# The values of self-attention in PE tiles of 64 rows by 32 columns

## Chip, cores and metric

The kernel runs on one core of a Trainium2 chip. The metric is device time in microseconds (us) of one execution, lower is better. All data is float32.

## What is computed

A transformer block over `x` of 2 x 1024 x 256: self-attention, cross-attention over a context of 154 tokens, and a gated feed-forward, each behind a layer norm and with a residual. There are 16 heads of width 64. Only the self-attention matters here:

```python
def _attention(xq, xkv, wq, wk, wv, wo, bo):
    q = (xq @ wq).reshape(B, S, N_HEADS, D_HEAD)
    k = (xkv @ wk).reshape(B, T, N_HEADS, D_HEAD)
    v = (xkv @ wv).reshape(B, T, N_HEADS, D_HEAD)
    attn = jnp.einsum("bihd,bjhd->bhij", q, k) * D_HEAD ** (-0.5)
    attn = jax.nn.softmax(attn, axis=-1)
    out = jnp.einsum("bhij,bjhd->bihd", attn, v).reshape(B, S, D_ATTN)
    return out @ wo + bo
h = _layernorm(x, ln1_g, ln1_b)
x = _attention(h, h, sa_wq, sa_wk, sa_wv, sa_wo, sa_bo) + x
```

## The kernel before

The order of all work is written out by hand, instruction by instruction and per engine; each engine works its own list in order and waits on semaphores.

**Units and slots.** Self-attention is cut into 16 units, each a pair of heads of one batch (`units`, L578). A unit has eight slots, 128 in all: the loop `for p in range(SA)` (L1036 to L1070) takes one slot per turn. In each slot TensorE does first two score tiles (`self_first`, L637, which calls `scores`, L476) and then one more piece of work from a list.

**Scores.** A score tile is 128 partitions x 2 heads x 512 keys in PSUM, `s`; the pool `ps_s` has two of them. The partitions are four groups of 32, for two groups of 32 queries and two halves of the keys. TensorE works here as eight small arrays (tiles) side by side, each of 64 rows by 32 columns: 64 rows because a head is 64 wide, two row groups for the two heads, four column groups for the four groups of partitions. The tile is set by `tile_position=(j * DH, a4 * KB)` (L486). The projections of queries and keys (`project_both`, L345, lines 352 in the profile, tiles `pq_sa`, `pk_sa`) have the same shape in this stage, since they are called with `m=KB`, 32 columns.

**Softmax.** DVE takes the negative maximum of a score tile (L645, `st`), ACT the exponentials with their sums (L494, `p`). The two halves of the keys exchange maxima and sums by small DMAs within SBUF (`exchange`, L500, `st<-st`), GpSimd joins them (`join`, L508, up to `den`), DVE takes the reciprocal (L591, `rd`) and GpSimd scales `p` with it (L595). DVE then transposes `p` in blocks of 32 x 32 into `pT` (L609, `turn_groups`, two slots later).

**The values weighed.** Four slots of a unit are followed by a call of `self_values` (L613), two for each half of the 1024 queries. It calls `weigh` (L523) for four of the eight tiles `t` of keys; two calls make one half. `weigh` multiplies the values `v` (stationary) with `pT` (moving, 256 queries at a time) and sums over all keys into two PSUM banks, `po[0]` and `po[1]`. Keys lie 64 to a row group (`a2`); `e` selects the copy of the values in which the two row groups are exchanged, so that each row group serves both banks' keys in turn. In the profile this is line 530, tiles `po`, `pT`, `v_sa`. ACT copies the finished banks to `o_sa` (L630).

**Other pieces.** The other four slots of a unit carry the projection of the next unit's queries (`pq_sa`), keys (`pk_sa`) and values (L383, `pv_sa`, tiles of 64 rows by 128 columns), and a piece of the output projection (L457, `py_sa`, whole array of 128 x 128). Transposes of layer norms (`ph_ln`) ride along in some slots. Self-attention ends near 713 us; cross-attention follows (its scores `sc`, L772, its values `poc`, L851, in tiles of 64 x 64), and the feed-forward (`pa`, L933, `pf`, L956). Two calls of `self_values` fall in the first slots of cross-attention (L1117 to L1120).

A call of `nc.tensor.matmul` on float32 data is recorded as two pairs of a weight load (LDWEIGHTS, row PEld) and a matmul (row PE): the 2048 calls of `weigh` are the 4096 loads and 4096 matmuls of line 530.

Of the kernel before, what the change touches and what calls it, by code (L numbers as in the profile page):

```python
# [18 lines left out]
def tile_transformer_block(ctx: ExitStack, tc: tile.TileContext, a: dict, out: bass.AP):  # L19
# [8 lines left out]
    DH = 64  # L28
# [11 lines left out]
    KB = 32  # L40
# [3 lines left out]
    QG = 2 * KB  # L44
    TP = NB * KB
    NM = P // QG
    QH = S // 2
    GH = QH // QG
    NK = HB // KB
# [45 lines left out]
    row_of, r = {}, 0  # L95
# [427 lines left out]
    def weigh(po, v, pT, t):  # L523

        for e in range(2):
            for a2 in range(2):
                r = slice(a2 * QG, (a2 + 1) * QG)
                n = 2 * t + (e ^ a2)
                for j in range(2):
                    nc.tensor.matmul(  # L530
                        po[a2][j * DH:(j + 1) * DH, :QH // 2],
                        lhsT=v[r, t, e, j * DH:(j + 1) * DH], rhs=pT[r, j * NK + n, :],
                        start=(t == 0 and e == 0), stop=(t == NT - 1 and e == 1),
                        tile_position=(a2 * QG, j * DH),
                    )


# [75 lines left out]
    def self_values(h, part):  # L613

        b, pr = units[h // 2]
        if part == 0:
            bank = sum_tile if h < 2 * NU - 1 else mm_tile
            halves[h, "po"] = [bank(f"po_{h}_{a2}") for a2 in range(2)]
            if pr % HP == 0 and h % 2 == 0:
                oT["sa", b, pr // HP] = pt_.tile([P, HP, S], F32, tag="oT", name=f"o_sa{b}_{pr}")  # L620
        po = halves[h, "po"]
        for t in range(NT // 2 * part, NT // 2 * (part + 1)):
            weigh(po, qk["sa", b, pr][2], halves[h], t)
        if part == 0:
            return None
        dst = oT["sa", b, pr // HP][:, pr % HP, (h % 2) * QH:(h % 2 + 1) * QH]

        def store():
            for a2 in range(2):
                nc.scalar.copy(  # L630
                    dst.rearrange("p (g a i) -> p g a i", a=2, i=KB)[:, :, a2, :],
                    po[a2][:, :QH // 2].rearrange("p (g i) -> p g i", i=KB),
                )

        return store
# [342 lines left out]
    with tc.manual_schedule():  # L978
# [57 lines left out]
        for p in range(SA):  # L1036
# [21 lines left out]
            if h == 0 or hg < LAG:  # L1058
# [4 lines left out]
                ui, n = divmod(p, 2 * SH)  # L1063
# [8 lines left out]
        for c in range(CA):  # L1072
# [13 lines left out]
            ui, n = divmod(c, len(CG))  # L1086
# [125 lines left out]
```

## Time and profile before

| What | us |
|---|---|
| median of 3 runs | 1120.16 (1119.69 to 1120.71) |
| the profiled execution | 1119.22 |
| its span, first to last instruction | 1117.4 |
| TensorE matmul busy | 1103.5 |
| VectorE (DVE) busy | 855.7 |
| ScalarE (ACT) busy | 629.5 |
| GpSimd (POOL) busy | 681.0 |
| line 530, matmuls of `po`, busy (4096) | 235.8 |
| line 483, matmuls of the scores, busy (4096) | 251.6 |

A row of the profile names line, engine, operation and tiles (written <- read). For TensorE it gives the shape of the PE tile first, rows*columns (64*64), and then partitions x elements of the moving operand (64x256). Behind the bar stand the busy time of the group in us, the mean length of one in ns, and the idle time of the engine just ahead of it with what ended it. Matmuls side by side in different tiles overlap, so the busy time of a group is far less than its count by its mean. The ends of matmuls are modelled; their starts are recorded, so the pace of TensorE is read from start to start. The granted TensorE clock was 1.00 over the whole span.

### The profile page before, as it was taken

What the parts mean: (1) busy time and instruction counts of PE and PEld (TensorE: products, weight loads), DVE (VectorE), ACT (ScalarE), POOL (GpSimd) and SP (SyncE); (2) the same over time, 40 slices, a digit from 0 to 9 for tenths busy, and PEclk for the clock granted to TensorE, in tenths of its full rate; (3) what the DMA queues carried; (4) which work ended last, traced back from release to release, by engine and by line L of the source; (5) the groups of instructions that cost most, each with busy time, mean ns of one, the idle gap of its engine ahead of it and who ended that gap; (6) DMA issues with size and microseconds to landing.
All of it is one profiled execution on the core that took longest, in us unless ns stands there. A gap on an engine that the chain in (4) does not pass through costs nothing.

```text
span 1117.4 us, 36668 instructions
## 1 busy us (share of the span) xinstructions
PE 1103.5 (99%) x14340; PEld 686.5 (61%) x14340; DVE 855.7 (77%) x1205; ACT 629.5 (56%) x2030; POOL 681.0 (61%) x1584
## 2 busy tenths in 40 slices
PE   8999999999999999999999999999999999999998
PEld 5445545545545455455455455476776777888887
DVE  4889999898998899999989989868777875412212
ACT  4666666766666666667666765665555553121111
POOL 2777777777777777777777777766656653220000
PEclk9999999999999999999999999999999999999999
DMA  3222212111111012011111111146665453000000
GB/s 85 70 57 50 55 27 51 48 34 41 32 31 42 22 41 46 13 42 39 24 41 32 31 32 26 25 95 158 160 157 125 114 115 79 10 11 10 20 10 19
DMA packets 102318, 59.14 MB, mean 53 GB/s; under 512 B 31994, under 2 KB 92930, under 8 KB 102146
## 3 DMA queue, kind: packets, MB, share of 16 engines
q1 hardware_dynamic: 100914, 56.15, 21.3%
q8 instruction: 113, 1.85, 0.7%
q10 hardware_dynamic: 1232, 0.66, 0.2%
q14 instruction: 59, 0.48, 0.1%
HBM read 27.12 MB, written 2.10 MB: 26 GB/s over the span
## 4 chain that ended last, share of the span: by engine, by line
PE 92%; ACT 2%; DVE 2%; DMA 1%; POOL 1%; SPq 1%; issue 1%; DVEq 0%; ACTq 0%; POOLq 0%
PE s L483 20%; PE po L530 20%; PE pa L933 10%; PE py_sa L457 5%; PE pv_sa L383 5%; PE py_ca L457 5%; PE pf L956 5%; PE pk_sa L352 4%; PE pq_sa L352 4%; PE pq_ca L352 4%; PE poc L851 4%; PE sc L772 3%; ACT p L494 2%; PE ph_ln L270 1%; PE pv_ca L733 1%; DVE st L645 1%
## 5 line engine op out<-in xcount | busy, mean ns | idle before, releaser
L494 ACT ACTIVATE p<-s,st 128x512 f32<-128x512 f32 x512 | 344.8, 686 | 199.0 <-DVE st L645 190.6
L595 POOL TENSOR_SCALAR p<-p,rd,ee 128x512 f32<-128x512 f32 x512 | 385.6, 768 | 47.6 <-DVE rd L591 46.3
L645 DVE TENSOR_REDUCE st<-s 128x2 f32<-128x1024 f32 x256 | 301.1, 1217 | 26.9 <-PE s L483 13.5
L609 DVE STREAM_TRANSPOSE pT<-p 128x1024 f32<-128x1024 f32 x256 | 302.2, 1218 | 0.3 <-POOL p L595 0.3
L483 PE MATMUL s<-k_sa,q_sa 64*32 64x512 f32 x4096 | 251.6, 594 | 5.0 <-ACT p L494 4.3
L530 PE MATMUL po<-pT,v_sa 64*64 64x256 f32 x4096 | 235.8, 380 | 0.9 <-DVE pT L609 0.9
L530 PEld LDWEIGHTS po<-pT,v_sa 64*64 64x64 f32 x4096 | 150.6, 133 | 109.3 <-issue 31.2
L483 PEld LDWEIGHTS s<-k_sa,q_sa 64*32 64x32 f32 x4096 | 66.8, 106 | 126.3 <-issue 68.2
L799 POOL TENSOR_SCALAR p<-p,rden 128x154 f32<-128x154 f32 x256 | 96.8, 399 | 76.0 <-DVE rden L796 75.6
L788 ACT ACTIVATE p<-sc,neg 128x154 f32<-128x154 f32 x256 | 96.1, 405 | 83.3 <-DVE rden L796 78.1
L942 DVE SCALAR_TENSOR_TENSOR u<-pa,cols,gate 128x256 f32<-128x256 f32 x64 | 31.0, 484 | 123.1 <-ACT gate L939 123.1
L933 PE MATMUL pa<-hT_ln,wf 128*128 128x256 f32 x512 | 121.1, 380 | 0.2 <-ACT p L788 0.2
L939 ACT ACTIVATE gate<-pa,cols 128x256 f32<-128x256 f32 x64 | 30.3, 474 | 147.8 <-PE pa L933 146.0
L933 PEld LDWEIGHTS pa<-hT_ln,wf 128*128 128x128 f32 x512 | 96.9, 190 | 13.9 <-issue 0.8
L494 ACT ACTIVATION_READ_ACCUMULATOR p<-s,st 128x1 f32 x512 | 103.8, 203 | 0.0
L383 PEld LDWEIGHTS pv_sa<-sa_wv,hT_ln 64*128 64x128 f32 x1024 | 58.8, 188 | 14.5 <-DMA st<-st 5.9
L518 POOL TENSOR_TENSOR zz<-ee,st 128x8 f32<-128x8 f32 x128 | 25.9, 202 | 65.6 <-ACT ee L516 65.6
L956 PE MATMUL pf<-wf,u 128*128 128x256 f32 x256 | 64.7, 379 | 0.0
L383 PE MATMUL pv_sa<-sa_wv,hT_ln 64*128 64x128 f32 x1024 | 62.0, 276 | 0.2 <-ACT v_sa L392 0.2
L457 PE MATMUL py_sa<-sa_wo,o_sa 128*128 128x256 f32 x256 | 59.7, 386 | 0.0
L457 PE MATMUL py_ca<-ca_wo,o_ca 128*128 128x256 f32 x256 | 59.7, 382 | 0.0
L457 PEld LDWEIGHTS py_sa<-sa_wo,o_sa 128*128 128x128 f32 x256 | 47.4, 190 | 17.8 <-issue 6.2
(87 smaller groups left out, 1250.6 us busy)
## 6 DMA issues: line engine op xcount, KB each, us to landing
wf<-pT_ca SPq DMA_DIRECT2D x128, 128.0 KB, 2.4
st<-st SPq DMA_DIRECT2D x512, 1.0 KB, 1.8
v_sa<-v_sa SPq DMA_DIRECT2D x32, 256.0 KB, 3.5
sa_wq<-in_L_xattn_sa_wq_dram SPq DMA_DIRECT2D x32, 128.0 KB, 2.8
sa_wk<-in_L_xattn_sa_wk_dram SPq DMA_DIRECT2D x32, 128.0 KB, 2.9
sa_wv<-in_L_xattn_sa_wv_dram SPq DMA_DIRECT2D x32, 128.0 KB, 2.9
ca_wq<-in_L_xattn_ca_wq_dram SPq DMA_DIRECT2D x32, 128.0 KB, 3.3
wf<-in_L_xattn_ff_w_dram SPq DMA_DIRECT2D x12, 256.0 KB, 4.2
```

What stands on the lines that cost most here:

```text
L352: nc.tensor.matmul(pq[r][f:f + m, at:at + n], lhsT=wt[own, c, f:f + m], rhs=h[own, c, t0:t0 + n], start=(c == 0), stop=(c == NH - 1), tile ...
L383: nc.tensor.matmul(pv[r][:, i * P:(i + 1) * P], lhsT=h[own, c, i * P:(i + 1) * P], rhs=wt[own, c, :], start=(c == 0), stop=(c == NH - 1), ...
L457: nc.tensor.matmul(py[:, e * D:(e + 1) * D], lhsT=o[:, i, (t + e) * P:(t + e + 1) * P], rhs=wo[kind][:, g * HP + i, :], start=(i == 0), st ...
L483: nc.tensor.matmul(sc[a4 * KB:(a4 + 1) * KB, j, :], lhsT=q[r, c:c + KB], rhs=k[r, h * HB:(h + 1) * HB], start=True, stop=True, tile_positi ...
L494: nc.scalar.activation(pr[:, j, :], sc[:, j, :], AF.Exp, bias=st[:, 0, 0, i, j:j + 1], accum_out=st[:, 0, 1, i, j:j + 1],)
L530: nc.tensor.matmul(po[a2][j * DH:(j + 1) * DH, :QH // 2], lhsT=v[r, t, e, j * DH:(j + 1) * DH], rhs=pT[r, j * NK + n, :], start=(t == 0 an ...
L595: nc.gpsimd.tensor_scalar(pr[:, j, :], pr[:, j, :], rd[:, c:c + 1], ee[:, 0, c:c + 1], op0=ALU.mult, op1=ALU.mult,)
L609: nc.vector.transpose(halves[h][:, :, c:c + KB], groups.pop(0).rearrange("p j (n k) -> p (j n) k", k=KB))
L645: nc.vector.tensor_reduce(st[:, 0, 0, i, :], sc[i], AX.X, ALU.max, negate=True)
L799: nc.gpsimd.tensor_scalar(pr_[:, j, i, :T], pr_[:, j, i, :T], rden[:, j, i:i + 1], 1.0, op0=ALU.mult, op1=ALU.mult,)
L933: nc.tensor.matmul(pa[:, half, :TF * P], lhsT=w1[:, c, half * DF + f * P:half * DF + (f + 1) * P], rhs=h[:, c, t0 * P:(t0 + TF) * P], star ...
L956: nc.tensor.matmul(sums[blk][i][:, :D], lhsT=sums[blk, "u"][:, f, i * P:(i + 1) * P], rhs=w2[:, f, :], start=(f == 0), stop=(f == NF - 1),)
```

## The change

Each call of `weigh` had stationary values of 64 rows by 64 columns, one head, and four tiles of the array were in use at once, 64*64. Now the 64 columns of a head are cut in two: a call takes 32 columns of `v`, streams the same `pT` of its head (`d // DH`), and writes 32 partitions of `po[a2]`. So there are twice as many calls, eight tiles of 64*32. The sums, the PSUM banks, the data and what comes before and after stay.

```diff
             for a2 in range(2):
                 r = slice(a2 * QG, (a2 + 1) * QG)
                 n = 2 * t + (e ^ a2)
-                for j in range(2):
+                for d in range(0, 2 * DH, KB):
                     nc.tensor.matmul(
-                        po[a2][j * DH:(j + 1) * DH, :QH // 2],
-                        lhsT=v[r, t, e, j * DH:(j + 1) * DH], rhs=pT[r, j * NK + n, :],
+                        po[a2][d:d + KB, :QH // 2],
+                        lhsT=v[r, t, e, d:d + KB], rhs=pT[r, d // DH * NK + n, :],
                         start=(t == 0 and e == 0), stop=(t == NT - 1 and e == 1),
-                        tile_position=(a2 * QG, j * DH),
+                        tile_position=(a2 * QG, d),
                     )
```

(`KB` is 32, `DH` 64, `QG` 64, `QH` 512, `NK` 16, `NT` 8.)

## The prediction

> **What bounds the kernel now.** I read the page first (sections 1, 4, 5), then the chain of waits between 400 and 440 us, then busy time by stretch, the waits of the self-attention stage, and the start of the first scores.
>
> ```profile
> PE 1103.5 (99%) x14340; PEld 686.5 (61%) x14340; DVE 855.7 (77%) x1205; ACT 629.5 (56%) x2030; POOL 681.0 (61%) x1584
> ...
> L645 DVE TENSOR_REDUCE st<-s 128x2 f32<-128x1024 f32 x256 | 301.1, 1217 | 26.9 <-PE s L483 13.5
> L609 DVE STREAM_TRANSPOSE pT<-p 128x1024 f32<-128x1024 f32 x256 | 302.2, 1218 | 0.3 <-POOL p L595 0.3
> L483 PE MATMUL s<-k_sa,q_sa 64*32 64x512 f32 x4096 | 251.6, 594 | 5.0 <-ACT p L494 4.3
> L530 PE MATMUL po<-pT,v_sa 64*64 64x256 f32 x4096 | 235.8, 380 | 0.9 <-DVE pT L609 0.9
> L530 PEld LDWEIGHTS po<-pT,v_sa 64*64 64x64 f32 x4096 | 150.6, 133 | 109.3 <-issue 31.2
> L483 PEld LDWEIGHTS s<-k_sa,q_sa 64*32 64x32 f32 x4096 | 66.8, 106 | 126.3 <-issue 68.2
> ```
>
> TensorE is busy 99% of the span and has almost no idle time before the changed line (0.9 us) or the scores (5.0). What the array does back to back sets the end; a busy array can still lose time inside its busy time, though. For that, the chain of waits (columns: start, length, engine, tile, line, matmuls):
>
> ```profile
> 16 pieces in order of time: start us, us, what
> ...
> 411.97 1.88 PE s L483 x32
> 413.85 3.43 PE pq_sa L352 x64
> 417.28 1.72 PE s L483 x32
> 419.00 3.43 PE pk_sa L352 x64
> 422.43 1.72 PE s L483 x32
> 424.14 3.62 PE po L530 x64
> 427.76 1.88 PE s L483 x32
> ```
>
> The same 32 score matmuls take 1.72 us behind a projection in the same 64*32 shape, and 1.88 behind `po`, which is in 64*64. And `po` itself takes 3.62 where `pq_sa`, with as many columns through each tile (8 x 512 against 16 x 256), takes 3.43. Round by round in the trace: score rounds (eight matmuls side by side) follow each other at 429 ns; the last before `po` lasts 566 and the first behind it 453. Rounds of `po` (four side by side) follow at 216; its first lasts 266, its last 325 to 327. So one visit to `po` costs 137 + 50 + 110 + 24 = 321 ns beyond its rounds, paid only at the change of shape: between scores and `pq_sa` or `pk_sa` every round is 428 to 430.
>
> **The change, part by part.** *Counts.* `weigh` makes 2048 calls, each recorded as two loads and two matmuls (4096 in the rows). After: 4096 calls, 8192 loads and 8192 matmuls, half as wide in weights, each still streaming 256 columns. A visit becomes 128 matmuls in 16 rounds of eight instead of 64 in 16 rounds of four. Banks, accumulation, the waits on `pT` and the ACT copies (L630) stay.
>
> *Removed.* The trace has 64 visits; 62 follow a score piece, 61 are followed by one. Gain: 62 x (137 + 50) + 61 x (110 + 24) = 11.6 + 8.2 = **19.8 us**. The two visits among the cross-attention scores still change shape; they keep their cost.
>
> *A round of eight with 256 columns* is not in the trace. Nearest row: `pq_sa`, also 64*32, eight tiles, also accumulating: 3.43 / 16 = 214 ns per 256 columns; `po` with four tiles of 256 columns now takes 216. Lower end 214 (2 us more gained), since eight streams never ran faster. Upper end: eight starts spread over 47 ns in a round, four over 20; were those 27 ns paid in every round, 992 x 27 = 27 us would be lost. Score rounds hide the 47 whole, so I take 216. One nanosecond per round is 1 us of the total.
>
> *Weight loads.* 8192 of 106 ns (row L483) instead of 4096 of 133. In score rounds the load for the next round starts 2 ns after its own tile's matmul and ends long before 216 ns: hidden. The Trainium skill ("TensorE: Matmul & The Clock Gate", Part 3, The mechanism) speaks against this: a load overlaps running matmuls only if the row group differs, and the new order puts four tiles of one row group in a row. By that rule a load of 106 ns would show in each round: 992 x 106 = +105 us. The trace has all eight loads running beside matmuls on both row groups, and the scores keep pace; I follow the row: nothing.
>
> *Issue.* 256 instructions must now pass in 3.45 us, 13.5 ns each; everything in the steady trace runs at 27 (16 per 429 ns, 8 per 216). The same page (Part 1, Wait — 56ns, not 53.3ns?) says matmul starts never come closer than about 25 ns. Applied to matmuls alone, 128 x 25 = 3.2 us still fits; applied to loads too, 6.4 us, +2.8 us per visit. Row against it, from the first scores, where the sequencer had stood still:
>
> ```profile
> 17.57 0.66 PE L483 MATMUL s<-k_sa,q_sa 64*32 64x512 f32 x8 [0.65 <-DVE k_sa L373]
> ```
> ```profile
> 17.54 0.21 PEld L483 LDWEIGHTS s<-k_sa,q_sa 64*32 64x32 f32 x16 [0.81 <-ACT k_sa L375]
> ```
>
> The 0.21 us of the sixteen loads end with one load of 0.106, so all started within 0.11 us, the eight matmuls among them, 77 ns behind the start of a semaphore instruction (17.47 us) that had held the queue empty: under 5 ns each. It is a burst of 31, not 256, so it bounds the sequencer and not a sustained supply. The supply: instructions come in 16 KB packets (113, 1.85 MB, 64 B each), 1.1 us of DMA per packet of 256 (0.7% of 16 x 1117 us), one needed per 3.45 us. I take nothing; the other end is a rival below.
>
> *What is late next.* DVE. It does two reductions and two transposes per score piece, 4 x 1.22 = 4.87 us, and a reciprocal of 0.17. A pair of scores and `po` falls from 5.49 us to 5.17.
>
> ```profile
> core 0: us, PE busy (x) PEld busy (x) DVE busy (x) ACT busy (x) POOL busy (x), PEclk, DMA share, GB/s
> ...
> 49.36:713.00 663.64, 661.51 (x10810) 347.00 (x10812) 605.28 (x675) 437.35 (x1293) 501.10 (x1120) 1.00 0.16 37
> ```
> ```profile
> PEld s L483 <- ACT p L494: 34.0, 81, 1.3
> ...
> DVE rd L591 <- POOL den L520: 29.6, 49, 1.6
> ```
>
> DVE is busy 605 of 664 us, and in some of its idle time it waits for `den` (30 us), which a faster TensorE does not remove. 605 + 30 = 635 leaves 29 us: enough for 19.8, though close. The new wait stands at the scores: their two PSUM tiles come free when ACT has made the exponents (L494), which wait for the reductions. Queued behind that wait are the scores themselves and, in order, the next `po` or projection. The trace gives the margin of each visit: from the end of the second tile's exponents to the next start on that tile, less 143 ns, the smallest seen. Of the 62 visits, eight have less than 321 ns; their shortfalls sum to 1.4 us. Taking savings of neighbouring visits together, until a slot in which ACT starts as early as it ever does (2.51 us behind the scores, DVE not behind), the shortfall is 7.5 us. The first ignores the queue on DVE, the second ignores idle time in which DVE catches up; I take the middle, **4.4 us** given back. Cover for it are the slots that stay long (`pv_sa` 5.65, `py_sa` 5.53).
>
> **Sum.** 19.8 - 4.4 = 15.4 us. Profiled execution 1119.22 us (span 1117.4 and 1.8 around it) becomes 1103.8; the median of the runs is 0.9 above the profiled one, so **1104.8**.
>
> **Rivals.**
> *Faster, mostly as worked out* (chance 0.73): 1099.5 to 1113. Low: all 19.8 and a little pace. High: shortfall 7.5 and 5 ns more in each round.
> *Faster by less* (0.06): 1113 to 1117.9; DVE becomes the bound, its queue never recovering between the long slots.
> *The change does not do what it says* (0.06, within 0.2%, 1118 to 1122.4, about 1120): a round of eight costs 20 ns more than one of four, and 992 x 20 = 19.8 cancels the gain. For: the wider spread of starts. Against: scores and projections hide it.
> *Slower: the supply of instructions* (0.15). Place: within the 62 visits. Break-even is 3.62 + 0.16 = 3.78 us for 256, 14.8 ns each; at 25 ns a visit takes 6.4 us, 2.6 us over break-even, +163 us: 1283. For: no steady stretch of the trace goes below about 27 ns; a queue filled beforehand can hide a slow sequencer in a burst. Against: that burst came from an empty queue, and 27 is just what the array's rounds allow. A smaller excess would land between.
>
> **Numbers.** 0.2% (2.2 us) is about what a measurement of this kernel can tell from no change. Faster 0.73 + 0.06 = 0.79, same 0.06, slower 0.15. The range 1099 to 1115 takes in the first case and part of the second, and leaves the last two out.
>
> **What would show it.** L530 as 64*32, 8192 matmuls, rounds near 216 ns; `po` at 3.45 us for 128 matmuls; scores at 1.72 behind `po`; the first two thirds of the span shorter, the rest unchanged. More waits of scores for L494 and a higher DVE share show what was given back. Wrong if `po` grows beyond 3.6 us (issue or loads), or if scores behind `po` stay at 1.88, so that the cost did not belong to the shape.

## The result and the profile after

The changed kernel takes 1112.51 us (median of four runs, 1111.62 to 1113.27) against 1119.93 for the kernel before in runs beside it: ratio 0.9935, interval 0.9918 to 0.9952. It is 7.4 us faster. The forecast was 15.4 us. The sign and the range hold; the size is less than half of what was forecast.

From the page after, the lines that answer to those shown of before:

```profile
PE 1093.7 (99%) x18436; PEld 733.5 (66%) x18436; DVE 855.1 (77%) x1205; ACT 628.2 (57%) x2030; POOL 681.4 (61%) x1584
...
PE 56%; ACT 11%; DVE 10%; POOL 8%; DMA 7%; issue 4%; SPq 4%; DVEq 0%; POOLq 0%; ACTq 0%
...
L645 DVE TENSOR_REDUCE st<-s 128x2 f32<-128x1024 f32 x256 | 300.9, 1216 | 20.3 <-PE s L483 7.1
...
L483 PE MATMUL s<-k_sa,q_sa 64*32 64x512 f32 x4096 | 262.1, 592 | 7.4 <-ACT p L494 6.5
L530 PE MATMUL po<-pT,v_sa 64*32 64x256 f32 x8192 | 239.5, 376 | 0.9 <-DVE pT L609 0.9
L530 PEld LDWEIGHTS po<-pT,v_sa 64*32 64x32 f32 x8192 | 177.9, 106 | 70.5 <-issue 22.0
```

The second line is the chain that ended last, by engine. On the page before it was

```profile
PE 92%; ACT 2%; DVE 2%; DMA 1%; POOL 1%; SPq 1%; issue 1%; DVEq 0%; ACTq 0%; POOLq 0%
```

TensorE held 92% of it before and holds 56% now; the rest has gone to ACT, DVE, GpSimd and DMA, though TensorE still shows 99% busy. (A score matmul is shown 592 ns long, and rounds follow each other at 429. A round that comes up to some 160 ns late leaves no idle time in the busy row; the chain shows it.)

What the change does on TensorE is what was worked out. The timeline of PE after, three pieces (start, length, matmuls):

```profile
403.06 1.92 PE L483 MATMUL s<-k_sa,q_sa 64*32 64x512 f32 x32
404.78 3.66 PE L530 MATMUL po<-pT,v_sa 64*32 64x256 f32 x128
408.23 1.92 PE L483 MATMUL s<-k_sa,q_sa 64*32 64x512 f32 x32
```

From start to start the scores take 1.72 us and `po` 3.45, where they took 1.88 and 3.62. Rounds of eight follow each other at 215 to 216 ns, the first and the last like the others. A slot without a stall is 5.17 us, 5.49 before.

But many slots stall. From the eighth slot of scores to the last, the kernel before takes 54.85 to 713.37 us, the changed one 54.94 to 704.57: 8.9 us less instead of 19.8. Cross-attention, from its first scores to the first matmul of the feed-forward, takes 208.05 instead of 206.78, 1.3 more: before, one of its first pieces waits (`po`, 0.89 us for `pT`); now `po` waits as long (0.88), and a piece of scores waits 1.01 us for an exponential as well. From there the two agree.

The waits of the self-attention stage after (49.36 to 704.57 us; total, times, longest):

```profile
PEld s L483 <- ACT p L494: 60.6, 111, 1.6
...
DVE rd L591 <- POOL den L520: 28.0, 53, 2.1
POOL dd L512 <- DMA st<-st: 26.9, 45, 2.2
```

The score loads' wait for the exponentials has nearly doubled (34.0 before). The wait of DVE for `den` has not grown. So the bare total of a wait doesn't tell what it costs: before, some 29 us of it cost little (leaving out the whole exchange gains that kernel 2.7 us, e5 below), and now they cost more. The chain between 405 and 435 us shows a stretch of it:

```profile
410.50 1.24 DVE st L645
411.76 1.16 ACT p L494 x3
...
415.01 0.21 POOL den L520
415.54 1.24 DVE st L645
...
420.58 1.24 DVE st L645
...
426.73 1.75 DMA st<-st
428.58 0.73 POOL x L310
...
431.10 1.24 DVE st L645
```

Read the starts of the reductions: 410.50, 415.54, 420.58: one slot each, 5.04 us. This is a loop: reduction, exponentials, `ee` behind them on ACT, `zz` and `den`, `rd` on DVE, and only then the next reductions, which stand behind `rd` in DVE's list although their scores are ready. Before, a slot with `po` took 5.49 and left 0.45 us in which a delay was made good; now it leaves 0.13.

The next two slots take 10.52 instead of 10.08. The chain goes over the exchange there, but the exchange isn't what was late. GpSimd's timeline:

```profile
425.61 3.01 POOL L595 TENSOR_SCALAR p<-p,rd,ee 128x512 f32<-128x512 f32 x4 [0.32 <-DVE rd L591]
428.58 0.73 POOL L310 TENSOR_TENSOR x<-x,sa_bo 128x256 f32<-128x256 f32 x1
429.28 0.20 POOL L512 TENSOR_TENSOR dd<-st 128x4 f32<-128x4 f32 x1
```

The DMA has landed at 428.48, GpSimd scales until 428.62, and then the addition of a bias (L310) stands ahead of the join in its list. It is this piece of 0.73 us that makes `den` late. In other slots it is the exchange. One of these in full, from the timeline after:

```profile
370.99 0.21 ACT L516 ACTIVATE ee<-dd 128x8 f32<-128x8 f32 x1
...
372.10 2.36 DVE L645 TENSOR_REDUCE st<-s 128x2 f32<-128x1024 f32 x2
...
376.39 0.20 POOL L512 TENSOR_TENSOR dd<-st 128x4 f32<-128x4 f32 x1 [1.30 <-DMA st<-st]
...
377.92 0.18 DVE L591 RECIPROCAL rd<-den 128x4 f32<-128x4 f32 x1 [1.19 <-POOL den L520]
...
378.22 1.23 DVE L645 TENSOR_REDUCE st<-s 128x2 f32<-128x1024 f32 x1
```

The exponentials whose numbers are exchanged end at 370.97. GpSimd can begin the join only at 376.39, having stood idle 1.30 us for the DMA; DVE stands idle 1.19 us for `den`, and the reductions start 6.12 us after those of the slot before. Of DVE's 53 waits for `den` in the stage, 35 (18.9 us) come behind such idle time of GpSimd for the DMA, and 17 (8.9 us) behind a bias addition or a piece of a layer norm that stood ahead of the join.

### The profile page after: what moved, and what is told of

It reads as the page before. It is cut to its first block, busy times and chain, and to the rows that moved or that the text cites. A ratio compares the mean times of both kernels' runs of the same rounds, so it can differ in the third digit from the quotient of the medians.

```text
span 1109.7 us, 44860 instructions
## 1 busy us (share of the span) xinstructions
PE 1093.7 (99%) x18436; PEld 733.5 (66%) x18436; DVE 855.1 (77%) x1205; ACT 628.2 (57%) x2030; POOL 681.4 (61%) x1584
## 4 chain that ended last, share of the span: by engine, by line
PE 56%; ACT 11%; DVE 10%; POOL 8%; DMA 7%; issue 4%; SPq 4%; DVEq 0%; POOLq 0%; ACTq 0%
PE pa L933 10%; ACT p L494 10%; PE po L530 8%; PE s L483 8%; DVE st L645 6%; DMA st<-st 6%; PE py_ca L457 5%; PE pf L956 5%; PE pq_ca L352 4%; PE poc L851 4%; SPq L504 3%; POOL p L595 3%; PE sc L772 3%; PE py_sa L457 2%; PE pk_sa L352 2%
## 5 line engine op out<-in xcount | busy, mean ns | idle before, releaser
L483 PE MATMUL s<-k_sa,q_sa 64*32 64x512 f32 x4096 | 262.1, 592 | 7.4 <-ACT p L494 6.5
L530 PE MATMUL po<-pT,v_sa 64*32 64x256 f32 x8192 | 239.5, 376 | 0.9 <-DVE pT L609 0.9
L530 PEld LDWEIGHTS po<-pT,v_sa 64*32 64x32 f32 x8192 | 177.9, 106 | 70.5 <-issue 22.0
L483 PEld LDWEIGHTS s<-k_sa,q_sa 64*32 64x32 f32 x4096 | 78.8, 106 | 115.2 <-ACT p L494 66.4
```

What stands on the lines that cost most here:

```text
L483: nc.tensor.matmul(sc[a4 * KB:(a4 + 1) * KB, j, :], lhsT=q[r, c:c + KB], rhs=k[r, h * HB:(h + 1) * HB], start=True, stop=True, tile_positi ...
L530: nc.tensor.matmul(po[a2][d:d + KB, :QH // 2], lhsT=v[r, t, e, d:d + KB], rhs=pT[r, d // DH * NK + n, :], start=(t == 0 and e == 0), stop= ...
```

## The experiments

Theory L: a loop of latency, from the reductions over the exchange and the join back to the reductions, has become the pace; what was gained on TensorE is lost there. (The join of a slot is made during the next one, so the way over the exchange takes two slots; the loop of 5.04 us over ACT takes one.) Rival T: DVE's work, which the prediction named, is too much for the shorter slots. All ratios are to the kernel before, measured beside each run. Several of these kernels leave something out of the computation; the text of each says what.

**The reciprocal moved to GpSimd (e1 with the change, e2 without).**

```diff
-            nc.vector.reciprocal(rd, den)
+            nc.gpsimd.tensor_tensor(rd, den, minus, ALU.pow)   # minus: four columns of -1.0
```

> Changed kernel, with the reciprocal rd moved from DVE to GpSimd (a power of -1 right behind den). Theory L (a loop of latency: reductions, exponentials, exchange by DMA, join, rd on DVE, and the next reductions queued behind rd's wait): the loop is cut, the scores hardly wait for the exponentials, and the whole 19.8 us of the shape appear: about 1101 us, 1099 to 1103. Rival T (DVE's throughput): DVE loses 128 x 0.17 = 22 us of work, of which 4 us at most come back: 1108 to 1111.

> The same move of rd to GpSimd, in the kernel before. Both theories: TensorE sets the pace there and its stalls sum to some 2.5 us, so 1117 to 1120 us. If it gains as much as the changed kernel does, the move is worth time by itself and tells nothing of the change.

Measured: 1171.4 and 1171.2 us, ratio 1.0455 (1.044 to 1.047) for both. Both theories missed, because I had put the power at the 0.2 us of its neighbours. It takes 1.03:

```profile
L597 POOL TENSOR_SCALAR p<-p,rd,ee 128x512 f32<-128x512 f32 x512 | 385.9, 769 | 13.4
L593 POOL TENSOR_TENSOR rd<-den,minus 128x4 f32<-128x4 f32 x128 | 132.2, 1033 | 10.0
```

(Two GpSimd groups of e1.) With it GpSimd paces a slot at 5.70 us in both kernels, and DVE waits for it with the transposes. This tells nothing of L or T. That both kernels are equal shows that TensorE's shape is worth nothing once another engine sets the slot.

**The exchange left out (e3 with the change, e5 without).** No `exchange(st)`; the join reads the half's own numbers twice.

> Changed kernel without the exchange of maxima and sums between the two halves of the keys (each half is normalised with its own sum, so the softmax is over half of the keys each); DVE's list is unchanged. Theory L: the 2 to 3 us of DMA leave the loop, den is ready before DVE asks for it: 1099 to 1103 us. Rival T: DVE has the same work, 1111 to 1113.

> The kernel before without the exchange between the halves of the keys (each half normalised with its own sum). Theory L: only the few stalls of the kernel before go, 2 to 3 us: 1117 to 1118, so that the change is worth its whole 19.8 us when the exchange is absent from both (1098.2 with the change). If the exchange held up the kernel before just as much, it would fall by 10 us or more, to about 1108.

Measured: 1098.24 us with the change (0.9804, 0.979 to 0.9818) and 1116.8 without (0.9969, 0.9957 to 0.9981). Both lie a little below the ranges of L. DVE has the same list as before. Without the exchange the change is worth 18.6 us, close to the 19.8 worked out for TensorE; with it, 7.4. T falls, and the place is the exchange. One part of L's forecast did not come: DVE still waits for `den` in e3 (49.36 to 690 us), as long in total as in the changed kernel, in more and shorter waits:

```profile
DVE rd L593 <- POOL den L522: 32.0, 97, 1.5
```

So here too the total of that wait is no measure of its cost.

**Half of the transposes left out (e4).**

```diff
-                halves[h][:, :, c:c + KB], groups.pop(0).rearrange("p j (n k) -> p (j n) k", k=KB)
+                halves[h][:, :NK, c:c + KB], groups.pop(0)[:, 0, :].rearrange("p (n k) -> p n k", k=KB)
...
-                        lhsT=v[r, t, e, d:d + KB], rhs=pT[r, d // DH * NK + n, :],
+                        lhsT=v[r, t, e, d:d + KB], rhs=pT[r, n, :],
```

> Changed kernel in which only the first head of each pair is transposed, and both heads' values are weighed with it: DVE loses half of the transposes, 256 x 0.6 = 150 us of work, a quarter of its load in self-attention. Theory L: the transposes stand where DVE waits for den anyway, so little changes: 1108 to 1112 us. Rival T: the queue on DVE is gone and the whole 19.8 us appear: 1099 to 1102.

Measured: 1111.41 us (0.992, 0.9908 to 0.9933), 1.1 us below the changed kernel. The waits of e4 from 49.36 to 690 us:

```profile
DVE rd L591 <- POOL den L520: 156.5, 118, 3.1
PEld s L483 <- ACT p L494: 65.2, 116, 1.9
```

and DVE's busy time in that stretch, e4 and then the changed kernel (columns: stretch, length, PE, PEld, DVE, ACT, POOL, clock, DMA share, GB/s):

```profile
49.36:690.00 640.64, 634.57 (x14446) 373.87 (x14452) 466.27 (x657) 424.71 (x1257) 488.77 (x1091) 1.00 0.17 38
```
```profile
49.36:690.00 640.64, 637.53 (x14500) 385.89 (x14504) 590.96 (x659) 427.01 (x1266) 490.08 (x1096) 1.00 0.17 39
```

DVE has 125 us less to do and waits 128 us more for `den` (28.0 to 156.5). Its work was not what held the slots; the relief turned into waiting. T falls here too; this is the sharpest evidence against the prediction's reading of DVE.

**`ee` between the exponentials of the two score tiles (e6).** ACT's order changed: two exponentials, `ee` of the last slot, two exponentials.

> Changed kernel with the small exponential ee of the last slot's join issued on ACT between the exponentials of the two score tiles instead of behind both. Theory L: where the DMA has landed by then, den comes 1.8 us earlier and DVE waits less; where it has not, ACT waits for it: a part of the 9 us still missing comes back, 1103 to 1109 us. Rival: if the DMA is what comes last in most slots, ACT's new wait takes what was gained: 1111 to 1116.

Measured: 1274.07 us (1.1379, 1.1359 to 1.1398). The rival's sign, with a size that neither expected. ACT now stands behind the join, and so behind the DMA, before the second tile's exponentials; its next exchange comes later for it:

```profile
ACT ee L516 <- POOL dd L514: 329.7, 128, 4.3
PEld s L483 <- ACT p L494: 243.2, 123, 3.7
POOL dd L512 <- DMA st<-st: 226.9, 126, 14.0
```

ACT waits for the join in all 128 slots, and in 126 of them GpSimd waits for the DMA: in this order the exchange has not landed when half of the next slot's exponentials are done.

**The exchange on two queues (e7: two and two; e12: three and one).**

```diff
-            nc.sync.dma_start(
+            (nc.scalar if a4 % 2 else nc.sync).dma_start(      # e12: if a4 == 3
```

> Changed kernel with the four DMAs of the exchange on two queues, two issued by SP and two by ACT. Theory L: their issue, 4 x 0.59 us one behind the other on SP, falls to 1.2 us; ACT pays two issues per slot. If ACT's issues are cheap: 1102 to 1107 us; if they hold ACT for 0.59 us each, it is no better than 1111.

> Changed kernel, correct in full, with three DMAs of the exchange issued by SP and the fourth by ACT. The exchange as the limit: the last issue comes 0.6 us earlier, at about 1.3 us behind the exponentials, and ACT pays one issue of 0.58 us instead of the two that made the even split slow: 1103 to 1109 us. If ACT's issue takes back what SP's saves, as in the even split: 1111 to 1116.

Measured: 1118.08 us for e7 (0.9986, 0.9978 to 0.9993), 1109.01 for e12 (0.9902, 0.9886 to 0.9919). An issue on ACT takes 0.57 us, much as on SP (0.59). In e7 the last issue comes 0.67 us behind the exponentials in the median instead of 1.94, but ACT's own small work, `ee` among it, falls behind: from `dd` to `ee` 0.96 us instead of 0.74. That this is why e7 loses was not tested by itself. One issue on ACT is a small net gain: e12 is 3.5 us below the changed kernel, at the upper end of its own forecast, though the two intervals just touch (0.9919 and 0.9918). It is the fastest kernel here that computes the whole block.

**One DMA in place of four (e11).**

```diff
-        for a4 in range(4):
-            o4 = a4 ^ 1
-            nc.sync.dma_start(
-                out=st[a4 * KB:(a4 + 1) * KB, 1], in_=st[o4 * KB:(o4 + 1) * KB, 0]
-            )
+        nc.sync.dma_start(out=st[:, 1], in_=st[:, 0])
```

> Changed kernel with one DMA of 128 partitions in place of the four of the exchange (each half of the keys gets its own numbers back, so it is normalised with twice its own sum): the wait for a landing stays, three issues of 0.59 us go from it. If the exchange is what comes last: 1099 to 1104 us, close to the 1098.2 without any exchange. If the loop over ACT is: 1109 to 1112.

Measured: 1095.86 us (0.9791, 0.9778 to 0.9804), 16.6 us below the changed kernel, with a landing still to wait for. Its waits from 49.36 to 690 us:

```profile
PEld s L483 <- ACT p L494: 15.8, 35, 1.2
DVE rd L587 <- POOL den L516: 5.2, 15, 0.5
```

GpSimd no longer waits for the DMA at all in that stretch, DVE waits 5 us for `den` instead of 28, and the chain is TensorE's again (93%). So one issue and a landing are in time; four issues in a row and a landing are not. In the stage the join starts 3.95 us behind the exponentials at the earliest, in both kernels, since GpSimd is scaling the slot before until about then. In the changed kernel the last of four is issued at 1.94 us in the median, which leaves 2.0 us for it to land; a landing takes 1.8 in the median, but up to 3.4. One DMA is issued at 0.06, and its longest landing of 3.0 is still in time. With four issues the join starts at 4.59 in the median and past 5.02 in a quarter of the slots, with one at 3.96 and 4.33. The loop over ACT and the bias additions are as they were in e11, so these alone don't hold the slots.

This is 3 us below the range forecast for the exchange, and 2.4 us below e3, which has no exchange at all. e3 has one more GpSimd instruction of 0.2 us in each join, which may be the reason; no run tells.

**`ee` made by GpSimd (e10).** `nc.scalar.activation(ee, dd, AF.Exp)` becomes `nc.gpsimd.tensor_scalar(ee, dd, 1.0, 1.0, op0=ALU.mult, op1=ALU.add)`.

> Changed kernel in which the exponential ee of the join is left out and 1 + dd made on GpSimd stands in its place (the two halves of the keys are weighed wrongly), so that den no longer queues on ACT behind the next slot's four exponentials. If the loop within one slot (reductions, exponentials, ee behind them, den, rd) is what holds the slots: 1098 to 1103 us. If the exchange (its issue and landing) is what comes last: 1108 to 1112.

Measured: 1117.43 us (0.9979, 0.9972 to 0.9985), slower than the changed kernel by 4.9 and so outside both. The waits behind ACT are gone: from the start of `dd` to that of `ee` it took 0.96 us or more in a quarter of the slots, and takes 0.79 at most in three quarters now. Nothing came back for it, which speaks against the ACT branch, as e11 does. In the median the step is longer, 0.78 instead of 0.74, and in the quickest quarter it grew from 0.72 to 0.78. Over 128 slots that would be some 8 us, enough for the loss (an estimate from these figures; why e10 costs 5 us was not tested).

**The supply of instructions (e8, e9).** Each score call is cut into four of 128 columns.

```diff
+        for f in range(0, HB, P):          # e9: outermost; e8: innermost, around the call
...
-                    sc[a4 * KB:(a4 + 1) * KB, j, :], lhsT=q[r, c:c + KB],
-                    rhs=k[r, h * HB:(h + 1) * HB], start=True, stop=True,
+                    sc[a4 * KB:(a4 + 1) * KB, j, f:f + P], lhsT=q[r, c:c + KB],
+                    rhs=k[r, h * HB + f:h * HB + f + P], start=True, stop=True,
```

> Changed kernel with each score matmul cut into four of 128 columns: 32768 instructions of scores instead of 8192, in rounds of eight, 16 instructions per about 109 ns, 6.8 ns each. Array's pace: rounds of 109 ns, and the kernel within 5 us of the changed one, 1110 to 1117. If instructions can't be supplied at that rate (rival of the prediction, whose limit then lies between 6.8 and 13.5 ns), scores grow to at least 2.5 us from 1.72 and the kernel to 1200 us or more.

> The scores in pieces of 128 columns as in the last call (1838.8 us), but with the pieces as the outer loop, so that eight neighbouring calls go to eight different tiles. Supply of instructions as the limit: both orders have the same count, so this one stays near 1840. Order as the limit[...]: rounds of eight come back and the kernel falls at least below 1300; whether a score slot reaches the array's 1.75 us shows if 6.8 ns per instruction can be kept up.

Measured: 1838.83 us for e8 (1.6426, 1.6402 to 1.6449) and 1269.54 for e9 (1.1329, 1.1312 to 1.1346). The same instructions in another order differ by 569 us. So e8's size fits the forecast for a short supply, and its cause is the order: with eight in a row for one tile, the trace of e8 shows stretches of single matmuls at 109 ns, one tile at work; in e9 rounds of seven and eight follow at 109 ns. And e9 shows the limit that the prediction feared. Its PE timeline:

```profile
603.40 1.50 PE L484 MATMUL s<-k_sa,q_sa 64*32 64x128 f32 x90 [0.25 <-issue]
...
607.34 0.66 PE L352 MATMUL pq_sa<-hT_ln,sa_wq 64*32 64x512 f32 x8 [0.65 <-issue]
```

TensorE runs dry behind no semaphore, 102 us in all. Instructions come to TensorE in packets of 256, which start to arrive every 3.8 us in the median of the stage, never closer than 3.3; that is 13 ns per instruction at best and 15 in the median. Each of these dry times in the stage ends 1.15 to 1.62 us after the end of a packet. In the changed kernel they come every 4.8 us in the median, and TensorE doesn't run dry for them: short bursts at 6.8 ns are met, a mean much under 13 ns is not.

## Why the prediction was right in kind and wrong in size

- *Removed: 19.8 us.* Right. Scores 1.72, `po` 3.45, and 18.6 us when the exchange is absent from both kernels.
- *A round of eight takes 216 ns.* Right; the 47 ns spread is hidden.
- *Weight loads.* Right: 8192 of 106 ns, hidden. The rule of the Trainium skill ("TensorE: Matmul & The Clock Gate", Part 3, The mechanism) that a load overlaps only another row group's matmuls does not hold here in the form used: the loads stay hidden with four tiles of one row group in a row. (The section also names a load into a background weight buffer. That would fit: each load starts some 2 ns behind the start of a matmul, while eight tiles run.)
- *Issue.* Right for this change: 256 instructions pass in 3.45 us. Matmuls start 27 ns apart on the mean, which the 25 ns of the same page's Part 1 (Wait — 56ns, not 53.3ns?) would still allow; in e9 128 in a row start 13.6 apart, which it would not. The rival was nearer than I held it: 13.5 ns per instruction is between the best (12.9) and the median (14.9) of what the packets of e9 brought. A visit together with its scores has 320 instructions in 5.17 us, 16 ns each, which leaves a little more room.
- *What is late next: DVE, 4.4 us given back.* This step failed, in its size and in its engine. The term measured 12.4 us (19.8 - 7.4), 10.9 in self-attention and 1.3 at the hand-over to cross-attention by the traces; and it was not DVE's work (e4: 125 us less of it changed 1.1 us), but the join that came late, mostly behind the four issues of the exchange (e11: 16.6 us). The step counted DVE's work and each visit's margin as they stood, took 29 us of free DVE time for room, and booked the wait for `den` as something a faster TensorE leaves as it is. That wait did stay at 28 us; but it stands in loops, of which the one over ACT takes 5.04 us, and the change cut the slot around it from 5.49 to 5.17. As I read it, the margins of the kernel before were made afresh in each slot by 0.45 us of slack, and with 0.13 a late `den` is carried on to the next slot. No run shows this carrying-on by itself.
- *The hand-over to cross-attention* was not in the sum at all.
- None of the rivals with another sign came true. That 1112.5 us still lies in the first case (up to 1113) is luck: its upper end was made of a shortfall of 7.5 us and of 5 ns more in each round. The rounds cost nothing, and the shortfall was 12.4.

Still open: why e10 costs 5 us, why some landings take 3 us and more, and whether fewer transfers help e11 beside fewer issues (it has a quarter of both).

## What to carry to other kernels

A change of the array's tile shape costs time that no row of the profile names; compare the same instructions behind a neighbour of the same shape and behind another. Before counting on such a gain, measure the loops that run over other engines, from one instruction to the same one a slot or two later, undisturbed: where little is left between that length and the new slot, small waits that were absorbed begin to count. And look at what the engine did just before a late instruction, not only at the chain: the chain named a DMA where a bias addition was in the way. Look in such a loop for the serial issue of several small DMAs on one queue, and put neighbouring matmuls in different tiles in the program's order.

## What the runs showed of the hardware beyond that

- Leaving the 64*32 shape for 64*64 and coming back cost 321 ns of TensorE per visit.
- A power on GpSimd takes 1.03 us for 128x4, a subtraction of the same size 0.20.
- The issue of a DMA of 1 KB within SBUF takes 0.59 us on SP and 0.57 on ACT; one of 4 KB took 0.51 on SP (e11).
- TensorE's instructions came in packets of 256, at best one per 3.3 us; in short bursts they started every 6.8 ns (16 in 109 ns).
- The same matmuls took 1838.8 us of the kernel's time with eight in a row for one tile, and 1269.5 with eight neighbours in eight tiles.
